# A four-layer graph network kernel: the row of exponentials of layer 2 spread over the partitions by two DMAs through memory in place of four TensorE transposes, with one more step and other turns

## The chip, the cores and the metric

The kernel runs on one core of one Trainium2 chip, in one launch. The metric is the device time in microseconds, from a median of several runs. Every time in this section and the next ones comes from the kernel before the change.

## The reference

64 graphs of 256 nodes with 256 features pass through four layers, each wrapped as `x = layernorm(x + layer(x))`. `adj` is symmetric, has ones on its diagonal, and all four layers mask with it. Everything is float32.

```python
# layer 0: attention of 4 heads, projection Wo, its own layernorm with gamma and beta
attn = softmax(where(adj == 0, -1e9, q @ k.T / 8)); out = layernorm((attn @ v) @ Wo.T + bo) * gamma + beta
# layer 1: attention of 8 heads on the normed input itself (q = k = v), then an MLP
x1 = x + softmax(where(adj > 0, n @ n.T / sqrt(32), -inf)) @ n ; out = x1 + gelu(layernorm(x1) @ W1 + b1) @ W2 + b2
# layer 2: graph attention; the scores are a sum of a row term and a column term
Wh = h @ W; s1 = Wh @ a[:256]; s2 = Wh @ a[256:]
out = softmax(where(adj > 0, leaky_relu(s1[:, None] + s2[None, :], 0.2), -9e15)) @ Wh
# layer 3: scores from one of four vectors, chosen by adj (only adj == 1 occurs here)
out = softmax(where(adj == 1, leaky_relu((h * a0) @ h.T, 0.2), -9e15)) @ h
```

In layer 2 the exponential of a leaky ReLU of a sum is a larger of two products of exponentials. The kernel drops a factor that cancels in the softmax and computes, with keys on the partitions and queries along the row, `e[key, query] = max(f[query] * g[key], h[key])`. So it needs `f`, one number for each query, laid out as a row that is the same on all 128 partitions. This row is what the change treats.

## The kernel before

**Tiles and stages.** Two graphs (G=2, 512 nodes) form a group, and there are 32 groups. A group's nodes lie as TB=4 blocks of P=128 partitions; N=256 is the number of nodes of a graph and QB=2 its blocks. `group(g)` is a Python generator that builds the group's instructions and yields between steps. Its steps are: load and mask (L904 on in the changed file, L900 before), `layer0` (projections, attention, and per graph a `behind` generator: the row of reciprocals `zs` goes out to memory and back as `rr`, L728 and L730; L732 multiplies it in; then the WoT matmuls, the addition L739, and two norms that end in `z` and `xb`), `layer1` (transposes of `z` at the start, attention, its own `behind` with the transposes of `oT` and L770/L773, transposes of `xb` with L586 as their eviction, the W1 matmuls with gelu L788), and `others`: `project` with W2 (eviction L699), `renormed` (result `xn`), `layer2` and `layer3`, each of the last two ending in `values_of` (L815, L816) and `renormed`.

**Order of the work.** Up to three groups are in flight (`AT_ONCE = 3`). Three strings of digits written out by hand, `FIRST`, `ORDER` (45 digits, once for each group in the steady state) and `LAST`, say which group takes its next step: a digit is the age of the group, 0 for the newest. On TensorE the instructions are chained in exactly this order by `in_order` (L519), so TensorE never does anything earlier than the turns say. On VectorE (DVE), ScalarE (ACT) and GpSimd (POOL) the instructions of the three groups are merged by a scheduler, and then each engine works through its own list in order. SP issues nearly all DMAs and also works in order: an issue that waits holds up those behind it. The last group runs its two graphs as two separate `others((i,))`, in turns.

**Layer 2** (`layer2`, L820). The group's `xn` is transposed to `xT` (8 transposes). The wx matmuls (L829) give `Wh` with three more columns, evicted by ACT (L830). L836 takes the exponential of these columns: `ex`, 128 partitions by 4 blocks by 3. L839 then makes the row: for each block, a TensorE transpose whose input is one column of `ex` broadcast along the row, so that all 128 output partitions receive the same 128 numbers. The four transposes fill one PSUM buffer `pt` of the pool `ps_m` (four buffers). L843 computes `max(f*g, h)` on DVE four times with `pt` as its input, into `e` (the profile calls its buffer qT); L845 multiplies by the mask. After a yield `values_of` runs the matmuls of `v` (this is `Wh`) and qT, and L815 and L816 divide and add.

**The steady period on TensorE**, read from the timeline, in order, with the profile's names: wx, xb transposes, ex transposes, WoT, W1 (4 matmuls), v,qT, W1 (8), xn transposes, W1 (4), z,xT (layer 3's scores), b2m, W2 (8), z transposes, W2 (8), ps<-xT (layer 1's scores), b2m, W2 (8), x transposes, W2 (8), ps<-xT, e,z, WqT, ps<-xT, e,z, WkT, ps<-xT, e,z, oT transposes, WvT, qT,kT (layer 0's scores), xn transposes, e,z, qT,kT, then e,v and ones twice with oT transposes, qT transposes, and xn,qT (layer 3's values). The profile shows each float32 matmul as two PE entries.

Of the kernel before, what the change touches and what calls it, by code (L numbers as in the profile page):

```python
# [8 lines left out]
F32 = mybir.dt.float32  # L9
# [7 lines left out]
P = 128  # L17
N = 256
D = 256
NC = D // P  # L20
G = 2
QB = N // P
TB = G * QB
# [10 lines left out]
AT_ONCE = 3  # L34


ORDER = "011225334342343542234235432323132121321132121"


FIRST = "0010000201000100213100110101000000100"  # L40
LAST = ("001142322312324311231243212120210102100210100031121201232001201321001010101012100010101102"
        "01021000001000010010000")
PREPARE = 2


# [355 lines left out]
def usual_input(ctx: ExitStack, tc: tile.TileContext, a: dict, out: bass.AP, flag: bass.AP):  # L401
# [7 lines left out]
    nc = tc.nc  # L409
# [6 lines left out]
    small = ctx.enter_context(tc.tile_pool(name="small", bufs=8))  # L416
    ps_s = ctx.enter_context(tc.tile_pool(name="ps_s", bufs=2, space=bass.MemoryType.PSUM))
    ps_m = ctx.enter_context(tc.tile_pool(name="ps_m", bufs=4, space=bass.MemoryType.PSUM))
    dram = ctx.enter_context(tc.tile_pool(name="dram", bufs=2, space=bass.MemoryType.DRAM))


    ident = const.tile([P, P], F32, name="ident")
# [96 lines left out]
    def in_order(ins):  # L519

        if on_pe:
            tc.add_manual_dep(ins.ins, on_pe.pop(),
                              mybir.DependencyInfo(mybir.DependencyClass.NoSync, mybir.DependencyReason.DATA),
                              reason="the order of the program")
        on_pe.append(ins.ins.name)

    def matmul(*args, **kw):
        in_order(nc.tensor.matmul(*args, **kw))  # L528

    def transpose(*args):  # L530
        in_order(nc.tensor.transpose(*args))  # L531
# [32 lines left out]
    def blocks_of(gs):  # L564
        return range(gs[0] * QB, (gs[-1] + 1) * QB)
# [11 lines left out]
    def transposed(src, scale=None, bias=None, gs=ALL):  # L577

        on = tokens(gs)
        dst = act.tile([P, NC, T], F32, name="xT")  # L580
        for c in range(NC):
            pt = to_psum(src, c, gs)
            if scale is None:
                nc.scalar.copy(dst[:, c, on], pt[:, on])  # L584
            else:
                nc.scalar.activation(dst[:, c, on], pt[:, on], AF.Identity, bias=bias[:, c:c + 1], scale=scale[:, c:c + 1])  # L586
        return dst
# [217 lines left out]
    def values_of(e, v, one, x, rs, gs, var=None):  # L805

        y = act.tile([P, TB, D], F32, name="y")
        for t in sorted(blocks_of(gs), key=lambda t: -(t % QB)):
            i, q = divmod(t, QB)
            po = ps_m.tile([P, one + 1], F32, name="pm")  # L810
            for kc in range(QB):
                matmul(po, e(i, kc, q), v[:, i * QB + kc, 0:one + 1],
                       start=kc == 0, stop=kc == QB - 1)
            r = rs[:, t:t + 1]
            nc.vector.reciprocal(r, po[:, one:one + 1])  # L815
            nc.vector.scalar_tensor_tensor(y[:, t, :], po[:, 0:D], r, x[:, t, 0:D], ALU.mult, ALU.add)  # L816
        yield
        return (yield from renormed(y, gs, var))

    def layer2(x, mask, gs):  # L820
        xT = transposed(x, gs=gs)
        yield

        wh = act.tile([P, TB, W], F32, name="v")
        nc.gpsimd.memset(wh[:, :, D + 3:D + 4], 1.0)
        for tb in blocks_of(gs):
            pm = ps_m.tile([P, D + 3], F32, name="pm")
            for c in range(NC):
                matmul(pm, xT[:, c, tb * P:(tb + 1) * P], wx[:, c, :], start=c == 0, stop=c == NC - 1)  # L829
            nc.scalar.copy(wh[:, tb, 0:D + 3], pm)  # L830
        yield


        ex = small.tile([P, TB, 3], F32, name="ex")
        at = slice(gs[0] * QB, (gs[-1] + 1) * QB)
        nc.scalar.activation(ex[:, at], wh[:, at, D:D + 3], AF.Exp)  # L836
        pt = ps_m.tile([P, G, N], F32, name="pm")
        for t in blocks_of(gs):
            transpose(pt[:, t // QB, t % QB * P:(t % QB + 1) * P], ex[:, t, 0:1].to_broadcast([P, P]), ident)  # L839
        e = act.tile([P, G, QB, N], F32, name="qT")  # L840
        for t in blocks_of(gs):
            i, kc = divmod(t, QB)
            nc.vector.tensor_scalar(e[:, i, kc, :], pt[:, i, :], ex[:, t, 1:2], ex[:, t, 2:3], ALU.mult, ALU.max)  # L843
        eg = e[:, gs[0]:gs[-1] + 1].rearrange("p g k q -> p (g k q)")
        nc.vector.tensor_tensor(eg, eg, mask[:, gs[0]:gs[-1] + 1].rearrange("p g k -> p (g k)"), ALU.mult)  # L845
        yield
        return (yield from values_of(lambda i, kc, q: e[:, i, kc, q * P:(q + 1) * P], wh, D + 3, x, small.tile([P, TB], F32, name="r"), gs))
# [37 lines left out]
    def group(g):  # L885
# [20 lines left out]
        def others(gs):  # L906

            yield from project(y, hT, w2, both, b2m, gs)
            x = yield from renormed(y, gs)
            x = yield from layer2(x, mask, gs)  # L910
            x = yield from layer3(g, x, mask, gs)
            i, j = g * G + gs[0], g * G + gs[-1] + 1
            nc.sync.dma_start(out[i:j].rearrange("b (q p) d -> p (b q) d", p=P), x[:, gs[0] * QB:(gs[-1] + 1) * QB, 0:D])
# [82 lines left out]
    def turn(g):  # L996
        done[g] += 1
        next(groups[g], END)
        if g == 0 and done[0] > PREPARE:
            next(preparing, END)  # L1000
# [3 lines left out]
    for period in range(len(groups)):  # L1004
        for age in ORDER:
            g = period - int(age)
            if g >= 0:
                due[g] += 1
                if due[g] > done[g]:
                    turn(g)  # L1010
    for back in LAST:
        turn(len(groups) - 1 - int(back))
# [16 lines left out]
    pm = ps_m.tile([P, 1], F32, name="pm")  # L1029
# [38 lines left out]
```

## Time and profile before

| | before |
|---|---|
| runs | 2661.43, 2663.03, 2664.40 us, median 2663.03 us |
| profiled execution | span 2658.2 us |
| lies outside the span, by the difference to the median | 4.8 us |
| PE, DVE, ACT, POOL busy | 2586.9, 1965.7, 1293.9, 592.3 us |
| one steady period (1225.00 to 1305.40 us) | 80.40 us, PE busy 80.03 us |
| 0 to 66.5 us | PE busy 43.31 us |
| 66.5 to 180 us | PE busy 103.97 us |
| 260 to 2520 us | PE busy 2249.92 of 2260 us |
| 2520 to 2658.2 us | PE busy 111.74 of 138.2 us |

PE is TensorE's matmul side, PEld its weight loads, SPq SP's queue. A row of a group of instructions has the line in the kernel, the engine, the operation, output and inputs by name, shapes, count, then the busy time in us and the mean ns of one, then the engine's idle time ahead of them and what ended most of it. In a timeline the columns are the start in us, the time until the last of the row's instructions ends in us, engine, line, operation, names, shapes and count; in brackets stands the idle time before the row and what ended it. Instructions on PE overlap: the difference between two starts is what a row costs, and its own time is longer. The page of this kernel has the line numbers of the file before; from L837 on the changed file's lines stand 4 later.

### The profile page before, as it was taken

The page shows a single profiled execution, that of the slowest core. Times are in us where ns is not written, and L with a number is a line of the kernel's source. Part 1 is how long each engine was busy: PE and PEld are TensorE (multiplying, and loading weights), DVE is VectorE, ACT ScalarE, POOL GpSimd, SP SyncE. Part 2 cuts the span into 40 slices and gives each one's busy share as a digit, 9 for nine tenths or more (in the row PEclk, how much of TensorE's full clock was granted, in tenths as well). Part 3 has the DMA queues.
Part 4 walks back from the last instruction along what each step waited for, and adds up shares of the span by engine and source line. Part 5 has one row for each costly group of instructions (what it writes and reads, how often), then busy time and mean ns, then how long its engine had stood idle before and what let it go on. Part 6 is the DMA issues. An engine that isn't in the chain of part 4 may idle for free.

```text
span 2658.2 us, 44921 instructions
## 1 busy us (share of the span) xinstructions
PE 2586.9 (97%) x16648; PEld 1761.5 (66%) x16648; DVE 1965.7 (74%) x6189; ACT 1293.9 (49%) x1997; POOL 592.3 (22%) x1145
## 2 busy tenths in 40 slices
PE   6899999999999999999999999999999999999996
PEld 3567667666667666666676666676676676676665
DVE  4667777777777777777777777777777777777774
ACT  3445544545545545545455544555445455445442
POOL 2112222222222222222222222222222222222121
PEclk8999999999999999999999999999999999999998
DMA  6001011001010000010010110110110101000000
GB/s 163 25 9 32 26 37 37 25 29 29 29 37 29 33 29 28 29 37 27 28 36 25 33 37 25 29 37 21 36 37 25 29 29 29 29 21 17 17 1 25
DMA packets 113393, 83.20 MB, mean 31 GB/s; under 512 B 44304, under 2 KB 112656, under 8 KB 113168
## 3 DMA queue, kind: packets, MB, share of 16 engines
q1 hardware_dynamic: 111552, 78.94, 10.1%
q8 instruction: 134, 2.20, 0.4%
q10 hardware_dynamic: 1360, 0.79, 0.1%
q0 software_dynamic: 256, 0.53, 0.1%
q14 instruction: 91, 0.75, 0.1%
HBM read 54.80 MB, written 17.04 MB: 27 GB/s over the span
## 4 chain that ended last, share of the span: by engine, by line
PE 71%; DVE 17%; POOL 9%; issue 2%; DMA 1%; ACT 0%; SPq 0%; DVEq 0%; POOLq 0%; ACTq 0%
PE pm L528 55%; PE ps L528 10%; PE pm L531 7%; POOL rstd L551 6%; DVE st L544 3%; DVE y L816 2%; DVE y L744 2%; DVE xn L559 2%; POOL ve L547 2%; DVE z L559 2%; DVE mv L545 1%; DVE xb L750 1%; DVE y L743 1%; DVE r L815 1%; POOL ve L549 0%
## 5 line engine op out<-in xcount | busy, mean ns | idle before, releaser
L613 DVE SCALAR_TENSOR_TENSOR e<-e,mask 128x256 f32<-128x256 f32 x1024 | 428.2, 483 | 130.7 <-ACT e L605 130.7
L605 ACT ACTIVATE e<-ps 128x1024 f32<-128x1024 f32 x384 | 371.9, 1020 | 196.2 <-PE ps L528 176.3
L528 PE MATMUL pm<-L_gnn_W,hT 128*128 128x256 f32 x2048 | 463.0, 379 | 0.0
L528 PE MATMUL pm<-xT,L_gnn_W 128*128 128x512 f32 x1024 | 455.2, 592 | 0.0
L528 PEld LDWEIGHTS pm<-L_gnn_W,hT 128*128 128x128 f32 x2048 | 384.5, 190 | 49.2 <-issue 0.7
L788 ACT ACTIVATE hT<-pm,b 128x512 f32<-128x512 f32 x256 | 176.7, 691 | 408.1 <-PE pm L528 408.0
L528 PEld LDWEIGHTS pm<-xT,L_gnn_W 128*128 128x128 f32 x1024 | 191.7, 190 | 203.4 <-issue 198.5
L544 DVE BATCH_NORM_STATS2 st<-y 128x6 f32<-128x256 f32 x768 | 301.1, 408 | 6.7
L551 POOL TENSOR_TENSOR rstd<-ve,mhalf 128x2 f32<-128x2 f32 (+1 forms) x384 | 298.4, 777 | 26.7
L559 DVE TENSOR_SCALAR xn<-y,mv,rstd 128x256 f32<-128x256 f32 x384 | 141.9, 411 | 178.9 <-POOL rstd L551 178.8
L547 POOL TENSOR_SCALAR ve<-mv 128x2 f32<-128x2 f32 x384 | 98.9, 257 | 741.0 <-DVE mv L545 738.8
L774 POOL TENSOR_TENSOR both<-y,xb 128x512 f32<-128x512 f32 x64 | 81.4, 1272 | 764.2 <-DVE y L773 764.2
L607 DVE TENSOR_TENSOR e<-e,mask 128x1024 f32<-128x1024 f32 x128 | 150.8, 1221 | 15.3 <-ACT e L605 15.3
L528 PE MATMUL ps<-xT 32*128 32x256 f32 x2048 | 148.0, 402 | 2.2 <-ACT e L605 1.3
L586 ACT ACTIVATE xT<-pm,beta,gamma 128x512 f32<-128x512 f32 x128 | 92.3, 770 | 104.4 <-PE pm L531 104.3
L528 PE MATMUL pm<-e,z 128*32 128x256 f32 x2048 | 142.4, 387 | 0.3
L528 PEld LDWEIGHTS ps<-xT 32*128 32x128 f32 x2048 | 93.2, 185 | 74.0 <-issue 66.8
L528 PE MATMUL pm<-e,v 128*32 128x256 f32 x2048 | 125.4, 384 | 8.0 <-DVE e L607 8.0
L528 PE MATMUL pm<-L_gnn_WoT,oT 128*128 128x256 f32 x512 | 121.2, 391 | 8.3 <-DVE oT L732 6.0
L528 PE MATMUL ps<-qT,kT 64*128 64x256 f32 x1024 | 128.0, 389 | 0.5 <-ACT e L605 0.5
L528 PE MATMUL pm<-xT,L_gnn_WqT 128*128 128x512 f32 x256 | 120.9, 616 | 3.7 <-ACT xT L584 3.7
L816 DVE SCALAR_TENSOR_TENSOR y<-pm,r,xn 128x256 f32<-128x256 f32 x256 | 120.9, 473 | 2.5
(138 smaller groups left out, 4059.1 us busy)
## 6 DMA issues: line engine op xcount, KB each, us to landing
x<-in_x SPq DMA_DIRECT2D x32, 512.0 KB
adj<-in_adj SPq DMA_DIRECT2D x32, 512.0 KB
rr<-lines SPq DMA_DIRECT2D x124, 128.0 KB
out<-xn SPq DMA_DIRECT2D x31, 512.0 KB
adjT<-adjb SPq DMA_TRANSPOSE x128
L_gnn_W<-in_L_gnn_W SPq DMA_DIRECT2D x2, 1024.0 KB
lines<-zs SPq DMA_DIRECT2D x62, 4.0 KB
rr<-lines POOLq DMA_DIRECT2D x4, 128.0 KB, 3.3
```

The lines of the kernel that those rows point to most:

```text
L528: in_order(nc.tensor.matmul(*args, **kw))
L531: in_order(nc.tensor.transpose(*args))
L544: nc.vector.bn_stats(st[:, q, :], src[:, t, 0:D])
L547: nc.gpsimd.tensor_scalar(ve[:, 0], mv[:, :, 1], EPS, None, ALU.add)
L551: nc.gpsimd.tensor_tensor(rstd, ve, mhalf[:, 0:k * QB].rearrange("p (k t) -> p k t", k=k), ALU.pow)
L559: nc.vector.tensor_scalar(dst[:, t, 0:D], src[:, t, 0:D], mv[:, q, 0:1], rstd[:, q:q + 1], ALU.subtract, ALU.mult)
L586: nc.scalar.activation(dst[:, c, on], pt[:, on], AF.Identity, bias=bias[:, c:c + 1], scale=scale[:, c:c + 1])
L605: nc.scalar.activation(e, ps, AF.Exp, scale=scale)
L607: nc.vector.tensor_tensor(e, e, mask.unsqueeze(1).to_broadcast([P, 2, QB * N]), ALU.mult)
L613: nc.vector.scalar_tensor_tensor(e[:, h, k], e[:, h, k], 1.0, mask[:, k], ALU.mult, ALU.mult, accum_out=sums[:, kc, c, j:j + 1])
L788: nc.scalar.activation(hT[:, f, :], pm, AF.Gelu, bias=b1[:, f:f + 1])
L816: nc.vector.scalar_tensor_tensor(y[:, t, :], po[:, 0:D], r, x[:, t, 0:D], ALU.mult, ALU.add)
```

## The change

L837 to L839 go: the PSUM buffer and the four transposes. In their place stand a DRAM tile `line` (TB by P, three buffers), a DMA from SP that writes the first column of `ex` into it (L838 of the changed file; 512 elements of 4 bytes), an SBUF tile `pt` (two buffers of 128 by 512), and a second DMA from SP that reads `line` back into all 128 partitions (L841; 256 KB landed). Then comes a `yield` that was not there, so that `layer2` has one step more. L843 and L845 become L847 and L849 and read `pt` from SBUF. The turns are others: `ORDER` has 46 digits in place of 45, and `LAST` is longer; `FIRST` stays. The rest of the kernel is unchanged.

```diff
-ORDER = "011225334342343542234235432323132121321132121"
+ORDER = "2120533421433454432533423324232133212123112112"
 FIRST = "0010000201000100213100110101000000100"
-LAST = ("001142322312324311231243212120212010102100210100031121201232001201321001010101012100010101102"
-        "01021000001000010010000")
+LAST = ("114200232233132431123123421212010210210020100131210012122312012101032010100011200011100001"
+        "10120100010012100010000000000")
...
         nc.scalar.activation(ex[:, at], wh[:, at, D:D + 3], AF.Exp)
-        pt = ps_m.tile([P, G, N], F32, name="pm")
-        for t in blocks_of(gs):
-            transpose(pt[:, t // QB, t % QB * P:(t % QB + 1) * P], ex[:, t, 0:1].to_broadcast([P, P]), ident)
+        line = dram.tile([TB, P], F32, name="line", bufs=3)
+        nc.sync.dma_start(line[at, :].rearrange("t p -> p t").unsqueeze(2), ex[:, at, 0:1])
+        pt = small.tile([P, G, N], F32, name="pt", bufs=2)
+        on = slice(gs[0] * N, (gs[-1] + 1) * N)
+        nc.sync.dma_start(pt.rearrange("p g n -> p (g n)")[:, on],
+                          line[at, :].rearrange("t p -> (t p)").unsqueeze(0).to_broadcast([P, len(gs) * N]))
+        yield
         e = act.tile([P, G, QB, N], F32, name="qT")
```

The steady period on TensorE becomes, read from the changed kernel's instruction lists: wx, **WoT**, **xb transposes**, W1 (4 matmuls), v,qT, **W1 (12)**, xn transposes, b2m, **W2 (16)**, **z,xT**, **z transposes**, b2m, W2 (8), ps<-xT, x transposes, W2 (8), ps<-xT, e,z, WqT, ps<-xT, e,z, WkT, ps<-xT, e,z, oT transposes, **xn transposes**, WvT, qT,kT, e,z, qT,kT, e,v and ones twice in a row, oT and qT transposes, xn,qT. Bold is what stands elsewhere than before. On DVE the list of a period is the same in its operations. Ahead of the WoT matmuls it has L732 for the first graph, the two L816 that remain, the second graph's `xb` (L559), and L732 for the second graph; then the xn scaling, L739, the xn scaling of the second graph, L739, L847 four times, L849. Both graphs' `rstd` products (L553, L554) stand ahead of both graphs' `z`, and the first graph's W2 eviction L699 with its statistics stands ahead of layer 3's maximum and mask (L877, L879). The second graph's L699 with its statistics and its xn stands between the first eight and the next eight L613. On SP the issues of a period are: lines and rr twice, line, pt, out, x, the adjacency transposes, adj; `line` and `pt` stand directly behind the second graph's `rr` and ahead of `out`.

More of the change, by code (lines that the diff above doesn't have):

```diff
@@ L34 @@
 AT_ONCE = 3
-ORDER = "011225334342343542234235432323132121321132121"
+ORDER = "2120533421433454432533423324232133212123112112"
 FIRST = "0010000201000100213100110101000000100"
-LAST = ("001142322312324311231243212120210102100210100031121201232001201321001010101012100010101102"
-        "01021000001000010010000")
+LAST = ("114200232233132431123123421212010210210020100131210012122312012101032010100011200011100001"
+        "10120100010012100010000000000")
 PREPARE = 2
```

## The prediction, made before the changed kernel was run

> **What bounds the kernel now.** I read the page first: span, busy shares and the slices.
>
> ```profile
> span 2658.2 us, 44921 instructions
> PE 2586.9 (97%) x16648; PEld 1761.5 (66%) x16648; DVE 1965.7 (74%) x6189; ACT 1293.9 (49%) x1997; POOL 592.3 (22%) x1145
> ...
> PE   6899999999999999999999999999999999999996
> ```
>
> TensorE (PE) is full in all slices but the first two and the last. So a change can win only what it takes off PE or out of PE's few gaps, and it loses whatever gap it opens. Second, the groups that the change touches, kept apart by shape:
>
> ```profile
> L531 PE MATMUL pm<-ident,ex 128*128 128x128 f32 x128 | 20.9, 284 | 0.7 <-ACT ex L836 0.7
> L843 DVE TENSOR_SCALAR qT<-pm,ex 128x256 f32<-128x256 f32 x128 | 60.7, 535 | 2.1 <-PE pm L531 2.1
> L559 DVE TENSOR_SCALAR xn<-y,mv,rstd 128x256 f32<-128x256 f32 x384 | 141.9, 411 | 178.9 <-POOL rstd L551 178.8
> L586 ACT ACTIVATE xT<-pm,beta,gamma 128x512 f32<-128x512 f32 x128 | 92.3, 770 | 104.4 <-PE pm L531 104.3
> ```
>
> The ex transposes keep PE busy for only 20.9 us of 2586.9. Third, the waits of PE between 300 and 2400 us hold one line:
>
> ```profile
> PE pm L531 <- DVE z L559: 7.7, 26, 0.3
> ```
>
> Fourth, one steady period (1225.00 to 1305.40 us, 80.40 us long, PE busy 80.03) on PE's timeline, which gives costs from start to start:
>
> ```profile
> 1225.11 0.65 PE L531 MATMUL pm<-ident,ex 128*128 128x128 f32 x4
> 1225.59 3.62 PE L528 MATMUL pm<-L_gnn_WoT,oT 128*128 128x256 f32 x16
> 1229.05 3.60 PE L528 MATMUL pm<-xT,L_gnn_W 128*128 128x512 f32 x8
> ...
> 1253.45 0.38 PE L531 MATMUL pm<-ident,z 128*128 128x128 f32 x2
> 1254.14 1.16 PE L531 MATMUL pm<-ident,z 128*128 128x128 f32 x6 [0.30 <-DVE z L559]
> 1255.13 3.62 PE L528 MATMUL pm<-L_gnn_W,hT 128*128 128x256 f32 x16
> ```
>
> Four ex transposes cost 1225.59 - 1225.11 = 0.48 us, not 4 x 0.284. The z transposes cost 1255.13 - 1253.45 = 1.68 us; eight other transposes (xb, 1304.56 to 1305.44) cost 0.88, so 0.80 us is lost at this wait, more than the 0.30 that the bracket names. Last, two rows of DVE, one of ACT, two of SP's queue:
>
> ```profile
> 1226.01 0.66 DVE L732 TENSOR_TENSOR oT<-oT,rr 128x512 f32<-128x512 f32 x1
> 1228.25 1.89 DVE L843 TENSOR_SCALAR qT<-pm,ex 128x256 f32<-128x256 f32 x4
> ```
>
> ```profile
> 1224.96 1.43 ACT L586 ACTIVATE xT<-pm,beta,gamma 128x512 f32<-128x512 f32 x2
> ```
>
> ```profile
> 1218.98 0.54 SPq L728 DMA_DIRECT2D lines<-zs  x1
> 1220.85 1.23 SPq L730 DMA_DIRECT2D rr<-lines  x2
> ```
>
> L732 for the second graph ends at 1226.67, and the second half of the WoT matmuls needs it at 1225.59 + 1.73 = 1227.32: 0.65 us to spare. Between the xb transposes' end (1225.11) and the first W1 matmul (1229.05) lie 3.94 us, in which L586's two evictions (to 1226.39) hide. SP issues rr 1.87 us after lines: that is its wait for the write to land.
>
> **What the Trainium skill says.** "DMA: Bandwidth & Descriptors", section "Two DMAs through the same engine are not ordered": a DMA that reads what another wrote has to be issued after a wait for the first one's semaphore. The trace agrees (the 1.87 us). The same page, section "Anatomy of one DMA", puts a fixed cost of about 2.0 us on a DMA, mostly the write's receipt, for GpSimd's path; from SP's queue the trace has 1.65 to 2.57 us for lines. It has no row for a DRAM write in elements of 4 bytes, which `line` is. "VectorE: DVE Perf Modes", section "Mode 2×_2P": a float32 tensor_scalar from SBUF gets two results a cycle, PSUM has one read port. The trace agrees: L559 from SBUF 411 ns, L843 from PSUM 535 ns, at the same size. "SBUF — State Buffer", section "SBUF: two separate sides": a DVE instruction with two SBUF inputs and a GpSimd one lock each other out. The trace agrees: one L613 took 2.57 us (from 1264.69, others 0.42) beside POOL's L717 (2.42 us from 1264.56).
>
> **The change part by part.** W is the start of a period's wx matmuls (1220.66 in the period above), V that of its v,qT matmuls.
>
> 1. *Ex transposes gone*: -0.48 us of PE a period. (32 times: 15 us.)
>
> 2. *z transposes later*: they now come after all of W1, half of W2 and the z,xT matmuls: V + 3.51 (v,qT) + 10.29 (12 W1 matmuls at 0.857) + 0.87 (xn) + 0.22 (b2m) + 6.9 (W2) + 2.62 (z,xT) = V + 24.4; before it was 1253.45 - 1232.48 = V + 21.0. DVE's z chain should end near V + 22. The gap of 0.80 goes. The second oT transposes, now later too, win some 0.07. Sum of 1 and 2: -1.35.
>
> 3. *WoT ahead of xb and without ex*: WoT's second half is due 0.88 + 0.48 us earlier, at W + 3.50 + 1.73 = W + 5.23. L732 ended at W + 6.01 before. DVE's new list puts some statistics and the first xn scaling (with its wait for POOL, 0.85) behind L732, but keeps xb's L559, the L816 and L732 for the first graph ahead of it; summing its rows from L641's end I get W + 4.9 to 5.6 for its end. I take the late end plus 0.06 for the semaphore: +0.40 us.
>
> 4. *xb directly ahead of W1*: nothing lies between any more. c=0's transposes take 0.44, its L586 about 0.77 and the ways between some 0.2, so W1 starts 1.42 + 0.06 after xb's start instead of 0.88: +0.60. Behind it nothing waits on c=1: one W1 matmul (0.857) covers the second L586.
>
> 5. *The two DMAs*: ex ends at W + 4.32 (before: 1225.05, W + 4.39). SP has nothing else to do by then: line is issued at W + 4.35. Landing seen +2.1 us (estimate; 1.65 to 2.57 for lines, and up to 3.0 since 512 elements of 4 bytes are unmeasured). Then pt's issue and landing: rr's first packets come 1.45 us after its issue, two of 128 KB each take some 3.2 us from the first issue; one of 256 KB at +2.4 (2.0 to 2.9). pt lands at W + 8.9 (8.0 to 10.3). DVE, behind L739 and the xn scalings, reaches L847 at W + 9.5; four at 0.33 (L559's steps: 0.73 - 0.41 = 0.32) and L849's 1.22 end at W + 12.1. v,qT is due on PE at W + 3.50 + 3.46 + 0.88 + 3.43 + 1.00 (points 3 and 4) = W + 12.27. So the DMAs are hidden, with a margin of about 0.6 us for the landing: 0 taken. Without that cover each us costs a us. Queued on SP behind the wait for line are out (next wanted with slack: before it was issued 6 us later than rr and waited for nothing on PE) and x of a later group: nothing. L847 is 4 x 0.12 us shorter than L843; DVE has idle time there: 0. pt is no PSUM buffer any more, so ps_m has one less taker: 0, no wait for a buffer shows in the waits of PE.
>
> 6. *Layer 1's scores*: ps<-xT comes at V + 28.96. ACT's exponential behind it (L605) waits for the adjacency's conversion, and that for DVE's mask L904, which now starts after z,xT's maximum and mask, shifted by the change to V + 24. I get L605 at V + 30.85, 1.9 us after ps<-xT; before 1260.83 - 1258.68 = 2.15. But e,z follows ps<-xT after 1.08 + 0.87 + 3.45 + 1.08 = 6.5 us now, and after 1268.93 - 1258.68 = 10.25 before (b2m and eight W2 matmuls have moved out from between). In 6.5 us lie L605 (1.02), eight L613 (2.8), and the lock by L717, which the x transposes release about 2 us after ps<-xT: 7.0 to 7.1 in all, with the last L613 needed only 0.4 before the end: 0.1 to 0.3. Then L699, statistics, POOL's power and xn (3.6 us by the rows from 1267.97) and eight more L613 stand ahead of the second e,z: about 0.75 in all, by the later of the two. Bounds 0 to 1.3.
>
> 7. *Smaller*: WvT behind xn's transposes waits for an eviction (0.1), xn,qT for ACT's L642 (0.05): +0.15.
>
> Sum of a period: -1.35 + 0.40 + 0.60 + 0.75 + 0.15 = +0.55 us. I count some 28 periods in the new order: +15 us. Head and tail: in the tail each of the last group's two parts exposes the pair of DMAs (4.5 us), but before stood there too with gaps of 26.5 us in 138; other turns fill some. The head swaps WoT and xb as well. I take 0, bounds -6 to +8. The profiled span would go from 2658.2 to 2673.2; the median lies 4.8 above the span: 2678.
>
> **The rivals.**
> *A: all covers hold.* z's gap and the ex transposes go, points 3, 4, 6, 7 cost nothing: -1.35 x 28 - 2 = -40, 2623; with half of these costs 2650. For it: PE is 97% busy and the turns seem laid out for just this order. Against: L586 has nothing between it and W1, which can't hide. Chance 0.20 (below 2658).
> *B: it evens out.* Point 6 doesn't arise, 3 and 4 do: -1.35 + 1.00 + 0.15 = -0.20, x 28 = -6; or half of point 6: +5. About 2657 to 2668. Chance 0.12 (within 0.2%).
> *C: the forecast*: 2668 to 2695. Chance 0.46.
> *D: pt lands too late.* The place is L847, behind the two DMAs in series. It decides from W + 9.5 on: if line takes 3.0 and pt 2.9, pt lands at W + 10.3, L849 ends at W + 12.9: +0.6 a period on top, 2695; another microsecond for scattered 4-byte writes makes 2723. Then DVE, working in order, holds the statistics behind L847 back as well. Against: spread evenly over the 16 DMA engines that is 32 elements each. Chance 0.22 (over 2695).
> *E: the change does nothing*: not possible, the transposes are out of the list.
>
> **How the numbers follow.** About 0.2% (5.3 us) is what a measurement can tell from no change. Faster: A, 0.20. Same: B, 0.12. Slower: C and D, 0.46 + 0.22 = 0.68. The range leaves out the better half of A (below 2645) and the worse third of D (above 2712). The slower cases alone: 2668 to 2712.
>
> **What would show it.** Right: the group ident,ex is gone; PE's wait for z is gone; a row WoT with idle time for L732 near 0.4 us; W1's first matmul 0.6 us behind xb, released by L586; e,z with waits for L613's e; pt landed before DVE is done with L739. Wrong: L847's idle time put down to a DMA, with v,qT waiting for L849 (D); no wait at e,z (B); a period below 80.4 us (A). The sum is most open to error in point 6 and in DVE's chain of point 3, where tenths are multiplied by 28.

## The result and the profile after

The changed kernel takes 3057.29 us in the median of four runs (3053.33 to 3059.18), against 2662.3 before (four runs, one more than in the table above): ratio 1.1482, interval 1.1466 to 1.1498. It is 395 us slower, where 15 were forecast. Its profiled execution has a span of 3051.5 us, 393.3 more than before. The same lines of the page that were read of the kernel before:

```profile
span 3051.5 us, 44685 instructions
PE 2668.6 (87%) x16520; PEld 1804.4 (59%) x16520; DVE 1955.3 (64%) x6189; ACT 1284.6 (42%) x1995; POOL 595.6 (20%) x1145
...
PE   6898998888988888988889988889888889888885
```

The chain that ended last, by engine:

```profile
PE 74%; DMA 16%; DVE 6%; ACT 2%; issue 1%; POOL 1%; SPq 1%; DVEq 0%; ACTq 0%; POOLq 0%
```

DMA had 1% of that chain before and has 16% now. The groups and the waits name the place: first a group of PE and one of DVE, then the four longest waits of PE over the whole span, then the wait of SP's queue for line:

```profile
L528 PE MATMUL pm<-v,qT 128*128 128x260 f32 x512 | 178.0, 521 | 276.3 <-DVE qT L849 276.3
...
L847 DVE TENSOR_SCALAR qT<-pt,ex 128x256 f32<-128x256 f32 x128 | 44.5, 408 | 278.1 <-DMA pt<-line 278.1
```

```profile
PE pm L528 <- DVE qT L849: 276.3, 32, 10.9
PE pm L528 <- DVE oT L732: 21.3, 7, 8.6
PE pm L528 <- ACT oT L640: 17.8, 29, 0.9
PE pm L528 <- ACT xT L586: 13.4, 32, 0.4
```

```profile
SPq L841 <- DMA line<-ex: 285.4, 33, 10.5
```

v,qT waits for L849 in nearly every group, L847 ahead of it waits for pt, and pt's issue waits for line's landing, that is, until the write is known to have arrived in memory. (Of the 21.3 us that PE waits for L732, only 0.7 lie between 300 and 2500 us.) The rows of v,qT and of the W1 matmuls behind it in a steady period before, then one steady period now on PE, SP and DVE:

```profile
1232.48 3.67 PE L528 MATMUL pm<-v,qT 128*128 128x260 f32 x16
1235.99 7.03 PE L528 MATMUL pm<-xT,L_gnn_W 128*128 128x512 f32 x16
```

```profile
1291.38 3.67 PE L528 MATMUL pm<-wx,xT 128*128 128x259 f32 x16
1294.88 3.61 PE L528 MATMUL pm<-L_gnn_WoT,oT 128*128 128x256 f32 x16
1298.34 1.04 PE L531 MATMUL pm<-ident,xb 128*128 128x128 f32 x8
1299.80 3.70 PE L528 MATMUL pm<-xT,L_gnn_W 128*128 128x512 f32 x8 [0.43 <-ACT xT L586]
1312.59 5.29 PE L528 MATMUL pm<-v,qT 128*128 128x260 f32 x16 [9.09 <-DVE qT L849]
1317.72 10.46 PE L528 MATMUL pm<-xT,L_gnn_W 128*128 128x512 f32 x24
```

```profile
1295.73 0.37 SPq L838 DMA_DIRECT2D line<-ex  x1
1304.89 0.34 SPq L841 DMA_DIRECT2D pt<-line  x1
```

```profile
1309.81 1.38 DVE L847 TENSOR_SCALAR qT<-pt,ex 128x256 f32<-128x256 f32 x4 [8.89 <-DMA pt<-line]
```

With W = 1291.38, line is issued at W + 4.35, as the prediction had it. SP can issue pt only at W + 13.5: line took 9.16 us to be seen, not 2.1. L847 starts 4.92 us after pt's issue, not 2.4. So v,qT is due at 1299.80 + 3.43 = 1303.23 and starts 9.36 us late. The gap costs more than its own length. Windows of PE over the gap, v,qT, and the W1 matmuls behind it (the columns are length, busy time of PE, PEld, DVE, ACT and POOL, granted clock of PE, DMA share, GB/s):

```profile
1300.00:1312.59 12.59, 3.50 (x8) 1.27 (x8) 3.52 (x7) 3.08 (x4) 0.10 (x1) 0.85 0.24 62
1312.59:1317.72 5.13, 5.13 (x17) 4.20 (x18) 2.41 (x8) 0.00 (x0) 0.00 (x0) 0.69 0.02 3
1317.72:1328.02 10.30, 10.30 (x26) 4.51 (x25) 7.26 (x27) 3.44 (x5) 4.08 (x9) 1.00 0.00 0
```

Behind the gap the granted clock is 0.69 and v,qT takes 5.13 us from start to start instead of 3.51 before. The Trainium skill describes this in "TensorE: Matmul & The Clock Gate", section "HAM oscillation — how this bites in real kernels": an engine that idles in a DMA's wait starts its next matmuls at a lower clock. The trace agrees: v,qT costs 1.62 us more a period, at a clock of 0.69.

**Where the 393 us lie**, by the starts of the wx matmuls of all groups. Up to the first group's +5.9; the 29 periods up to the thirtieth group's +352.9, typically 92.2 in place of 80.33 us each; from there to the end, with two more groups behind, +34.6 (186.7 against 152.1). The period that begins at 1291.38, 92.21 us long, against the one of 80.33 before (from wx to wx; the 80.40 used so far is the length of the window, not of the period) adds up so, from start to start on the two timelines: gap at v,qT +9.36, lower clock +1.62, W1 behind xb +0.58, the e,z +0.93, qT transposes and xn,qT +0.78, z transposes -0.81, ex transposes -0.48, oT transposes -0.10: +11.88, measured +11.88. (WvT +0.10, and smaller differences that cancel it, are left out.)

### The profile page after: what moved, and what is told of

Its sections match the earlier page's. It is cut to its first block, busy times and chain, and to the rows that moved or that the text cites. A ratio compares the mean times of both kernels' runs of the same rounds, so it can differ in the third digit from the quotient of the medians.

```text
span 3051.5 us, 44685 instructions
## 1 busy us (share of the span) xinstructions
PE 2668.6 (87%) x16520; PEld 1804.4 (59%) x16520; DVE 1955.3 (64%) x6189; ACT 1284.6 (42%) x1995; POOL 595.6 (20%) x1145
## 3 DMA queue, kind: packets, MB, share of 16 engines
q1 hardware_dynamic: 133216, 87.40, 10.6%
## 4 chain that ended last, share of the span: by engine, by line
PE 74%; DMA 16%; DVE 6%; ACT 2%; issue 1%; POOL 1%; SPq 1%; DVEq 0%; ACTq 0%; POOLq 0%
PE pm L528 58%; PE ps L528 11%; DMA line<-ex 10%; PE pm L531 5%; DMA pt<-line 5%; DVE qT L847 1%; DVE qT L849 1%; DVE e L613 1%; DMA rr<-lines 1%; POOL rstd L551 1%; ACT oT L640 1%; ACT v L830 0%; DVE st L544 0%; SPq L901 0%; DMA adj<-in_adj 0%
## 5 line engine op out<-in xcount | busy, mean ns | idle before, releaser
L613 DVE SCALAR_TENSOR_TENSOR e<-e,mask 128x256 f32<-128x256 f32 x1024 | 417.4, 471 | 169.3 <-ACT e L605 168.7
L528 PE MATMUL pm<-v,qT 128*128 128x260 f32 x512 | 178.0, 521 | 276.3 <-DVE qT L849 276.3
L528 PEld LDWEIGHTS pm<-v,qT 128*128 128x128 f32 x512 | 135.0, 271 | 331.1 <-issue 301.1
L559 DVE TENSOR_SCALAR xn<-y,mv,rstd 128x256 f32<-128x256 f32 x384 | 141.2, 410 | 167.5 <-POOL rstd L551 167.4
L847 DVE TENSOR_SCALAR qT<-pt,ex 128x256 f32<-128x256 f32 x128 | 44.5, 408 | 278.1 <-DMA pt<-line 278.1
L547 POOL TENSOR_SCALAR ve<-mv 128x2 f32<-128x2 f32 x384 | 89.9, 234 | 674.8 <-DVE mv L545 660.3
L528 PE MATMUL pm<-e,z 128*32 128x256 f32 x2048 | 170.0, 386 | 3.0 <-DVE e L613 2.4
L586 ACT ACTIVATE xT<-pm,beta,gamma 128x512 f32<-128x512 f32 x128 | 92.7, 778 | 135.9 <-PE pm L531 135.9
L528 PE MATMUL pm<-L_gnn_WoT,oT 128*128 128x256 f32 x512 | 127.3, 400 | 23.7 <-DVE oT L732 21.3
L796 POOL MEMSET xn<- 128x4 f32 x99 | 10.4, 106 | 696.3 <-DVE y L816 315.4
```

Source lines behind the costliest of these rows:

```text
L547: nc.gpsimd.tensor_scalar(ve[:, 0], mv[:, :, 1], EPS, None, ALU.add)
L559: nc.vector.tensor_scalar(dst[:, t, 0:D], src[:, t, 0:D], mv[:, q, 0:1], rstd[:, q:q + 1], ALU.subtract, ALU.mult)
L613: nc.vector.scalar_tensor_tensor(e[:, h, k], e[:, h, k], 1.0, mask[:, k], ALU.mult, ALU.mult, accum_out=sums[:, kc, c, j:j + 1])
```

## The experiments

Two theories stood at the start. L: the loss is the landing of line and pt, whatever the turns. T: the new turns themselves open the gap. Within L there are three finer ones: L1, each 4-byte element has its price; L2, the price is that of the bytes or of any write of this kind; L3, small writes that fall close together in memory hold each other up. In all kernels "line" is the time from SP's issue of line to its issue of pt, and "pt" from that to the start of L847 where pt ended the wait: medians over the steady periods, which move by up to 0.1 us with the choice of the first and the last period. turns_only, line_16_bytes_old_turns, line_16_new_turns and line_16_bytes_covered were executed four or five times, every other kernel once: of their totals only differences of tens of us are used. The edits are shown shortened.

**turns_only**: the changed kernel's turns and step, the row by TensorE transposes.

```diff
-        line = dram.tile(...); nc.sync.dma_start(line ...); pt = small.tile(...); nc.sync.dma_start(pt ...)
+        pt = ps_m.tile([P, G, N], F32, name="pm")
+        for t in blocks_of(gs):
+            transpose(pt[:, t // QB, t % QB * P:(t % QB + 1) * P], ex[:, t, 0:1].to_broadcast([P, P]), ident)
         yield
```

> The changed kernel's turns and its extra step, but the row is still made by four TensorE transposes into PSUM, standing between WoT and xb. Theory L (the landing of the two DMAs is the loss): no wait for L849 at v,qT, the small costs of the turns stay (about 0.6 us at W1, 0.9 at the two e,z, 0.6 at xn,qT, against 0.8 won at z), so 80.4 + 1.3 = 81.7 us a period and about 2700 us, at most 2720. Rival T (the turns themselves open the gap at v,qT): over 2850 us, with a wait of several us at v,qT.

Measured: 2748.28 us, ratio 1.0323 (1.0306 to 1.0341). T falls as the main cause: the turns alone cost 87 us and not 395, and v,qT waits for nothing. But the sum for L was too low by 1 us a period (82.65, not 81.7). The waits of PE between 300 and 2400 us show why:

```profile
PE pm L528 <- DVE y L739: 32.9, 25, 1.3
PE pm L528 <- ACT oT L640: 15.1, 25, 0.6
```

W1's matmuls wait 1.3 us for L739, the eviction of WoT: with pt back in PSUM, it seems, the four buffers of ps_m are taken at this place. That wait belongs to this mixture of the two kernels. The changed kernel doesn't have it.

**dma_old_turns**: the two DMAs in the turns of before, without the extra yield.

```diff
-ORDER = "2120533421433454432533423324232133212123112112"
+ORDER = "011225334342343542234235432323132121321132121"
 # LAST of before as well
...
                           line[at, :].rearrange("t p -> (t p)").unsqueeze(0).to_broadcast([P, len(gs) * N]))
-        yield
```

> The two DMAs in the turns of the kernel before, without the extra step. Theory L: line takes about 9 us and pt about 5 from issue to the reader, whatever the turns; v,qT is due 11.8 us after the start of wx here and qT is ready about 21 us after it, so 9 to 10 us a period are lost at v,qT, plus the lower clock behind the gap: 3040 to 3100 us, much as the changed kernel. Rival T: with the old turns the loss goes, below 2750 us.

Measured: 3047.24 us, line 10.47 and pt 3.50, a wait at v,qT of 9.56 us in the period at 1299 us. L holds: the old turns lose as much. On SP's list out now stands between line and pt:

```profile
1282.45 0.37 SPq L838 DMA_DIRECT2D line<-ex  x1
1285.72 0.39 SPq L916 DMA_DIRECT2D out<-xn  x1
1293.05 0.33 SPq L841 DMA_DIRECT2D pt<-line  x1
```

Its issue isn't what holds pt, which follows 7.33 us later. Whether out's transfer adds the 1.4 us over 9.09 was not tried.

**line_16_bytes**: 128 elements of 16 bytes in place of 512 of 4.

```diff
-        ex = small.tile([P, TB, 3], F32, name="ex")
+        ex = small.tile([P, 3, TB], F32, name="ex")
...
-        line = dram.tile([TB, P], F32, name="line", bufs=3)
-        nc.sync.dma_start(line[at, :].rearrange("t p -> p t").unsqueeze(2), ex[:, at, 0:1])
+        line = dram.tile([P, TB], F32, name="line", bufs=3)
+        nc.sync.dma_start(line, ex[:, 0, :])          # a part of the last group writes its half
```

> ex is laid out with its four blocks side by side, so that line is written as 128 elements of 16 bytes in place of 512 of 4; pt is read back as before, and L847 reads it with a stride. Theory L1 (the cost goes with the number of small writes, about 15 ns each beyond some 1.7 us): line is seen landed after 1.7 + 128 x 0.014 = 3.5 us instead of 9, the period falls by about 5.5 us plus some of the clock, to 86 us, and the kernel to about 2850. Rival L2 (the cost is in the bytes or in the wait for a write to DRAM as such): line still takes 8 to 9 us, no gain.

Measured: 2739.79 us; line 1.44, pt 3.87. One period on SP and PE:

```profile
1261.24 0.35 SPq L840 DMA_DIRECT2D line<-ex  x1
1262.66 0.34 SPq L842 DMA_DIRECT2D pt<-line  x1
```

```profile
1269.91 3.74 PE L528 MATMUL pm<-v,qT 128*128 128x260 f32 x16 [0.91 <-DVE qT L851]
```

Of the 395 us, 317 are gone. L2 falls: the bytes are the same. The landing is even shorter than L1's 3.5 us. Some 0.9 us of wait stay at v,qT; part of it is that the four multiplications that read pt with a stride take 1.77 us here, against 1.38 in the changed kernel.

**rows_by_transpose**: one transpose on TensorE makes four rows, which go out in four pieces of 512 bytes.

```diff
+        pr = ps_m.tile([TB, P], F32, name="pm")
+        transpose(pr, ex[:, at, 0], ident)
+        row = small.tile([TB, P], F32, name="row", bufs=2)
+        nc.scalar.copy(row, pr)
-        nc.sync.dma_start(line[at, :].rearrange("t p -> p t").unsqueeze(2), ex[:, at, 0:1])
+        nc.sync.dma_start(line[at, :], row)
```

> One TensorE transpose turns the four columns of ex into four rows of 128, ACT evicts them, and line is written as four pieces of 512 bytes. Theory L1: line is seen landed after 1.7 to 2 us, as lines is; with the transpose and its eviction (0.8 us) the chain is 6.5 us shorter than in the changed kernel, so the wait at v,qT falls from 9.1 to 2.5 us and the kernel to some 2790 us. pt: 4.9 us if its own landing is slow, 3 us if only because it reads what has just been written in small pieces. Rival L2: line still takes 8 us.

Measured: 2960.97 us; line 2.52 (out is issued right ahead of it), pt 3.25. The landing is near what L1 said, the total isn't: line is issued at W + 9.6 instead of W + 4.35. The transpose stands behind WoT in PE's order, so that the row is evicted at W + 7.6, and then line stands behind out on SP, which waits for DVE's xn until W + 9.1. v,qT still waits 6.01 us. A short DMA that is issued late delays its reader as a long one does.

**line_half**: 256 elements of 4 bytes instead of 512.

```diff
-        nc.sync.dma_start(line[at, :].rearrange("t p -> p t").unsqueeze(2), ex[:, at, 0:1])
+        half = slice(at.start, (at.start + at.stop) // 2)
+        nc.sync.dma_start(line[half, :].rearrange("t p -> p t").unsqueeze(2), ex[:, half, 0:1])
```

> The changed kernel, but line is a DRAM tile filled with ones once, and only the first half of its blocks is written for each group: 256 elements of 4 bytes in place of 512 (the other graph's row stays ones, so that part of the computation is left out). Theory L1 (each element of 4 bytes costs some 15 to 20 ns behind a fixed 1.4 us): line is seen after 5.0 to 5.5 us instead of 8.9. Rival L2 (a fixed 9 us for this kind of write): still 8.5 to 9.

Measured: 3035.34 us; line 7.89, pt 4.94. Neither theory: half the elements save 1.2 us of 9.1. The price isn't proportional to the number.

**line_4_bytes_adjacent**: line_16_bytes's places in memory, written as 512 elements of 4.

```diff
-        ex = small.tile([P, 3, TB], F32, name="ex")       # of line_16_bytes
-        nc.sync.dma_start(line, ex[:, 0, :])
+        ex = small.tile([P, TB, 3], F32, name="ex")
+        nc.sync.dma_start(line.unsqueeze(2), ex[:, :, 0:1])
```

> As line_16_bytes, with line laid out so that the four numbers of a partition stand side by side in memory, but ex keeps its layout, so that they are 512 elements of 4 bytes again. Only number and size of the elements differ from line_16_bytes, not the places written. L1 (number of elements): 8.5 to 9.5 us until line is seen. Rival L3 (the places: neighbours in memory written from different partitions): as in line_16_bytes 1.4 us, or near it, since each 16 bytes now come from one partition.

Measured: 2978.6 us; line 6.82, pt 4.29. That four neighbours come from one partition helps a little (9.09 to 6.82), and doesn't save it: at the same places, 128 elements of 16 bytes take 1.44. Neither L1's 8.5 to 9.5 us nor the 1.4 of this form of L3 came.

**line_64_apart**: 512 elements of 4 bytes, each 64 bytes from the next.

```diff
-        line = dram.tile([TB, P], F32, name="line", bufs=3)
-        nc.sync.dma_start(line[at, :].rearrange("t p -> p t").unsqueeze(2), ex[:, at, 0:1])
+        line = wide.pop()                       # one of three [TB, P, 16] DRAM tiles, filled with ones
+        nc.sync.dma_start(line[at, :, 0:1].rearrange("t p s -> p t s"), ex[:, at, 0:1])
```

> The changed kernel, but each of the 512 elements of 4 bytes goes to a place 64 bytes from the next, in a DRAM tile filled with ones; pt reads the first 2 KB of that tile, so its row is mostly ones and that part of the computation is left out. L1 (number of elements): line is still seen after about 9 us. Rival L3 (writes of less than a burst to the same piece of memory hold each other up): 1.5 to 3 us, the wait at v,qT falls to about 2 us.

Measured: 2722.97 us; line 1.93, pt 3.20. SP's queue and v,qT in one period (from L433 on, this kernel's lines stand 6 later, so that L855 is the multiplication by the mask):

```profile
1008.62 0.38 SPq L844 DMA_DIRECT2D wide<-ex  x1
1010.59 0.34 SPq L847 DMA_DIRECT2D pt<-wide  x1
```

```profile
1016.72 3.75 PE L534 MATMUL pm<-v,qT 128*128 128x260 f32 x16 [0.23 <-DVE qT L855]
```

The same 512 elements of the same size, in the same turns, are seen 4.7 times as fast once they don't lie next to each other. This decides for L3 in its wider form: closeness counts, and not only between partitions. (That the DRAM tile is one of three made ahead isn't the reason: line_half has such tiles too and takes 7.89.) In the changed kernel all 512 packets begin within 0.37 us (the trace's records of packets: 1296.63 to 1297.00), and 7.9 us pass until SP moves on: the time lies behind the start of the last packet, not in issuing them.

**line_16_apart**: the same at a distance of 16 bytes.

```diff
-        lk = dram.tile([TB, P, 16], F32, name=f"wide{k}", bufs=1)
+        lk = dram.tile([TB, P, 4], F32, name=f"wide{k}", bufs=1)
```

> As line_64_apart, but the 512 elements of 4 bytes stand 16 bytes apart, so four of them share 64 bytes in place of one (line_64_apart: 1.93 us) or sixteen (the changed kernel: 9.09 us). Its pt reads mostly ones, so that part of the computation is left out. L3 with 64 bytes as the piece and a cost for each further write to it: about 1.9 + 3/15 of 7.2 = 3.4 us until line is seen. If the piece is smaller than 16 bytes: 1.9 us; if it is a larger one (512 bytes and more) that both spacings shared: between 1.9 and 9 by no rule that I have.

Measured: 2743.34 us; line 2.71, pt 3.25. With 1, 4 and 16 elements to 64 bytes line takes 1.93, 2.71 and 9.09 us. The price rises with the density, slowly at first. How large the piece of memory is in which they disturb each other these three don't tell: whether one counts per 64 bytes or per 512, the curve is the same.

**later_values**: the DMAs of the changed kernel, v,qT behind all W1 matmuls.

```diff
-ORDER = "2120533421433454432533423324232133212123112112"
+ORDER = "2120533421433233345544233422321332121243112112"
```

> The changed kernel's DMAs as they are, but other turns: v,qT stands behind all 16 W1 matmuls (10.3 us later), and layer 3's scores further back. If the wait for pt is all that the DMAs cost, it goes (qT is ready 21 us after the start of wx, v,qT due at 22): no gap of several us and no lowered clock at v,qT, a period of 81 to 84 us, and a kernel of 2680 to 2780 us. Rival: DVE, which works in order, passes the wait on to the norms behind L847, and the period stays above 88 us.

Measured: 3145.69 us, slower still, some 95.6 us a period. PE's timeline at v,qT and z, and DVE's row of the wait:

```profile
1264.05 3.67 PE L528 MATMUL pm<-v,qT 128*128 128x260 f32 x16
...
1278.72 0.63 PE L531 MATMUL pm<-ident,z 128*128 128x128 f32 x2 [1.72 <-DVE rstd L554]
1282.16 0.87 PE L531 MATMUL pm<-ident,z 128*128 128x128 f32 x2 [2.81 <-DVE z L559]
```

```profile
1259.41 0.41 DVE L847 TENSOR_SCALAR qT<-pt,ex 128x256 f32<-128x256 f32 x1 [6.72 <-DMA pt<-line]
```

v,qT no longer waits and runs at full clock. But L847 still stops DVE for 6.72 us, and what stands behind it in DVE's list comes late, z first of all. The rival was right about the period, and its reason is seen in part: an engine that works in order hands a wait on. How much of z's delay comes from L847 this run doesn't tell, because v,qT's later place delays L815 and L816, which stand ahead of z's chain on DVE (line_16_bytes_covered shows that effect without a wait of this length).

**line_16_bytes_old_turns** and **line_16_new_turns**: the short landing in the turns of before, and in turns made for it.

```diff
-ORDER = "2120533421433454432533423324232133212123112112"   # line_16_bytes
+ORDER = "011225334342343542234235432323132121321132121"    # line_16_bytes_old_turns, with LAST of before, no yield
+ORDER = "2120533414323345442533423243213233212121132121"   # line_16_new_turns
```

> line written as 128 elements of 16 bytes, with the turns of the kernel before and no extra step. The landing is 1.4 us and pt's 3.5 to 4, so qT is ready some 12.6 us after wx starts, where v,qT is due at 11.3: a wait of about 1.3 us at v,qT against 0.48 won from the ex transposes; a period of 81.2 us, 2680 to 2695 us in all. If the turns of the changed kernel were the better ones for such a row it would come out above its 2740 us with line_16_bytes.

> line written as 128 elements of 16 bytes, and turns made for it from those of the kernel before: xb ahead of WoT again, v,qT one step of W1 later (so that it is due 14.8 us after wx starts), oT between the last two e,v as before, and layer 3's scores between the first two halves of W2. If every wait is covered the period is 80.33 - 0.48 = 79.9 us, or 79.1 with z's wait gone, and the kernel with the changed kernel's tail about 2650 to 2665. If z or e,z come to wait: 80.5 to 82 us, 2670 to 2710.

Measured: 2844.18 us (ratio 1.0685, 1.0668 to 1.0701) and 2744.99 us (1.0314, 1.03 to 1.0328). Neither came out as expected. In both, the scheduler puts out between line and pt on SP, and out waits for DVE's xn. SP's queue of the former:

```profile
1209.98 0.35 SPq L840 DMA_DIRECT2D line<-ex  x1
1213.24 0.39 SPq L918 DMA_DIRECT2D out<-xn  x1
1213.69 1.17 SPq L842 DMA_DIRECT2D pt<-line  x1
```

pt is issued 3.70 us after line instead of 1.44, and takes 4.4. v,qT waits 4.20 us in the old turns, behind which its clock falls too. In the turns made for it that wait is 0.64, but z still waits, and the x transposes wait 1.06 for L699, which reads the PSUM buffer that they need. The changed kernel's list has pt ahead of out: its turns did do something for the DMA.

**line_16_bytes_covered**: out on ACT's queue, v,qT one W1 step later, else the turns of before.

```diff
-ORDER = "011225334342343542234235432323132121321132121"
+ORDER = "011225334342334542233425342323132121321132121"
...
-            nc.sync.dma_start(out[i:j] ...
+            nc.scalar.dma_start(out[i:j] ...
```

> line_16_bytes_old_turns with its two causes of delay taken away: out is issued from ACT's queue, so that it no longer stands between line and pt on SP's, and in ORDER v,qT comes one W1 step (3.43 us) later, with the first half of W2 between xn and layer 3's scores in place of W1; FIRST and LAST are those of the kernel before. line 1.4 us and pt 3.9 after it: qT is ready 12.7 us after wx starts, v,qT is due at 14.8, so no wait there and full clock. If the TensorE time of the ex transposes (0.48 us a period) is a gain once all is covered: 79.9 us a period, about 2647 us. My theory of what is late next: z's transposes keep their place in the sum of work, so they only come 0.48 us earlier while DVE's chain up to z starts from the WoT matmuls as before: z's gap grows from 0.80 to 1.28 and the period stays 80.3, 2660 to 2675 us with a tail that still exposes the two DMAs.

Measured: 2826.95 us (1.0616, 1.0601 to 1.063). line 1.43, pt 3.92, no wait at v,qT. The only wait of PE between 300 and 2500 us, where it stands, and the windows of PE over z and over the W2 matmuls behind it:

```profile
PE pm L531 <- DVE z L559: 83.8, 52, 2.8
```

```profile
1238.66 0.72 PE L531 MATMUL pm<-ident,z 128*128 128x128 f32 x2 [0.41 <-DVE z L559]
1242.19 1.72 PE L531 MATMUL pm<-ident,z 128*128 128x128 f32 x6 [2.81 <-DVE z L559]
1243.71 5.45 PE L528 MATMUL pm<-L_gnn_W,hT 128*128 128x256 f32 x16
```

```profile
1238.09:1243.71 5.62, 2.33 (x11) 1.58 (x9) 3.88 (x15) 2.30 (x3) 1.44 (x3) 0.72 0.09 33
1243.71:1249.09 5.38, 5.38 (x18) 4.17 (x17) 1.51 (x3) 0.95 (x2) 0.00 (x0) 0.66 0.01 3
```

The place that I named, z, is what is late next; its size isn't as I said: the z transposes take 1243.71 - 1238.09 = 5.6 us (1.68 before; 1238.09 is where z,xT's share ends), and the clock falls behind them (W2 5.38 in place of 3.45). What I left out: DVE has the four L815 and L816 of v,qT ahead of z's chain, so v,qT's delay of 3 us arrives there too. No version with the row through memory came out below the kernel before.

## Why the prediction was wrong, by its own steps

The side was right, the size was not: 15 us were forecast and 395 measured.

- **Step 5, the two DMAs, is the one that failed.** It took 2.1 us for line (at most 3.0) and 2.4 for pt (at most 2.9); measured 9.09 and 4.91. Its points ahead of and behind the landings were right: line is issued at W + 4.35, and DVE is done with L739 at W + 9.5. But pt, which was to be there at W + 8.9, keeps L847 waiting until W + 18.4, and v,qT starts 9.4 us late where 0 was taken. The bound on line from above was the error. The nearest row, lines, writes four pieces of 1 KB; line writes 512 pieces of 4 bytes packed side by side, and I widened the row's figure by half instead of asking what such a write could cost at worst. Rival D named the right place, the point from which it decides and the order on DVE behind L847, and its price was far too small: it put pt's landing at W + 10.3, or 11.3. The Trainium skill's "DMA: Bandwidth & Descriptors", section "Specifications", says that below 512 bytes a DMA does read-modify-write; I argued from the count of elements (32 for each DMA engine) and not from that sentence. The runs here agree only in part: 512 elements of 4 bytes set apart land in 1.93 us, so smallness alone costs little, and packing them costs the other 7.
- **Step 5's "each us costs a us"** was too low as well: the gap of 9.36 us brought another 1.62 a period by the lower clock behind it. No term of the sum had that.
- **Steps 1 and 2** were right: -0.48, and -0.81 for z and -0.10 for oT (forecast -0.80 and -0.07).
- **Step 3** (WoT, +0.40): 0. WoT takes 3.46 us; L732 ends at W + 4.92, the early end of the span that I gave, and I had taken the late one. So v,qT was due 0.4 us earlier than step 5 reckoned, at W + 11.85, ahead of the W + 12.1 at which step 5 itself had L849 done: v,qT would have waited a little even with the landings that it assumed. (W itself was 1220.73 before, not 1220.66; nothing hangs on it.)
- **Step 4** (W1 behind xb, +0.60): +0.58, released by L586, as forecast.
- **Step 6** (e,z, +0.75): +0.93, at the two e,z named and released by L613's e.
- **Step 7** (+0.15): WvT +0.10 as forecast, but xn,qT +0.78, behind ACT's L640. In the new turns both e,v and ones stand directly behind each other, and oT's transposes no longer between them, so there is less work of PE between the second e,v, which L640 evicts, and xn,qT; that this is the reason is read from the order, not tried. I had put 0.05 on L642 and nothing on L640.
- **Head and tail at 0**: +5.9 and +34.6. line_64_apart, with short landings, has +4.2 and +4.2: some 30 us of the tail are the two DMAs of the last groups and parts.
- **Were the landings near those forecast**, line_64_apart tells about what would have come: 2722.97 us, a period of 81.9. That is 45 over the forecast. In most of its periods L847 no longer waits for pt: it starts at W + 9.6 and the mask is done at W + 12.3, nearly as step 5 had it, and v,qT starts at W + 12.4, 0.5 late (step 3's 0.4). With xn,qT's 0.8 that makes most of the rest. So the sum of the small terms was too low too, in the same direction.

Shown are: that line's and pt's landing holds v,qT (the waits, and line_16_bytes and line_64_apart, in which its wait falls from 9 us to 0.9 and 0.2); that density, not number or size alone, makes line slow; that the turns aren't the main cause (turns_only, dma_old_turns), though they cost tens of us of their own. Only argued, not tried by itself: that pt is slow for what line's writes leave behind. It takes 4.91, 4.94 and 4.29 us behind packed 4-byte writes, and 3.20 to 3.25 behind spread ones and rows of 512 bytes; behind the 16-byte writes it takes 3.87, in between. But the spread versions read mostly bytes that were not just written, and in dma_old_turns pt takes 3.50 behind packed writes. The traces say how this fits: there pt is issued 10.5 us after line. In the changed kernel too, the four steady periods in which line takes over 10.5 us have a pt of 3.5 to 3.6, those in which line takes under 9.4 one of 4.7 to 5.3, and line and pt together take about 14.0 us in nearly all. A read that is issued later finds less of the delay left. Left open is the size of the piece of memory in which the writes collide.

## What to carry to other kernels

Cost a DMA by how its pieces lie at the far end: their size and how close they stand. A column of single numbers that goes to adjacent addresses in DRAM is the bad case here (9.1 us for 2 KB); give each partition's numbers a contiguous run first (128 pieces of 16 bytes: 1.4 us). If no row of the profile has such a DMA, one and a half times the nearest row is no upper bound.

When four transposes on a full engine cost 0.48 us of 80, the most that their removal can bring by itself is 0.6%, while the chain of two dependent DMAs took 5 us at best here, which has to be covered on every in-order queue that it touches: SP's (out between line and pt, or ahead of line) and DVE's (all behind L847). What isn't covered costs TensorE its length, and behind the gaps of several us here 1.6 to 1.9 us more by the clock.

## What the runs showed of the hardware

- The same 512 writes of 4 bytes take 1.93, 2.71 or 9.09 us until the next DMA may be issued, at distances of 64, 16 and 4 bytes in DRAM; 256 of them at 4 bytes 7.89.
- A read of 2 KB into 128 partitions behind packed writes can start late as well: its first packet comes 2.41 us after the issue where it is issued 9.16 us after them, and 0.99 where it is issued 10.6 us after them (dma_old_turns); behind spread writes 0.98.
- A gap on TensorE costs more in the matmuls behind it, and not in proportion to its length: 1.6 us behind 9.1 (granted clock 0.69), 1.8 behind 4.2 in line_16_bytes_old_turns (0.68), 1.9 behind 3.3 us of idling within 5.6 at z in line_16_bytes_covered (0.66), and 0.1 behind 0.9 in line_16_bytes (1.00).
